# Order of the sums and the statistics in a merge stage, and the first line scan's write-back split by image

## The chip, the cores and the metric

The kernel runs on one core of a Trainium2 chip. Its time is the device time of one execution, in microseconds (us); the figure given for a kernel is the median of several runs. The engines are named as in the profile: PE is TensorE's matrix multiplication (PEld its weight load), DVE is VectorE, ACT is ScalarE, POOL is GpSimd, SP is SyncE, whose queue here issues most transfers (DMA).

## The reference

Four layers work on an fp32 image `x` of shape (2, 128, 128, 128): 2 images, 128 channels, 128 lines, 128 columns. Each normalises its input in groups of 4 channels and adds its result to it. Cut to what matters here:

```
x = x + attention(gn(x))        # layer 0: axial attention, its two outputs scaled, shifted and summed
x = x + scans(gn(x))            # layer 1: four line scans one after the other
x = x + deform_conv(gn(x))      # layer 2
x = x + hadamard_conv(gn(x))    # layer 3

def one_scan(x, w, vertical, reverse):          # layer 1 calls it for down, up, right, left
    def step(carry, xi):
        y = xi + relu(conv1d(carry, w))         # 128 to 128 channels, 9 taps along the line
        return y, y
    _, ys = scan(step, xs[0], xs[1:])           # line by line: each needs the line before it

def gn(v):                                      # mean and variance of 4 channels of one image
    return (g - mean(g)) / sqrt(var(g) + eps)
```

A scan is a chain of 127 steps, each of which depends on the step before. Layer 1's normalisation needs the mean and variance of the whole image that layer 0 leaves, so its first line can't start until the last part of layer 0's sum is there.

## The kernel before, in words

An image stands in SBUF with its 128 channels on the 128 partitions and its lines and columns in the free dimension. Both images are in one tile, `both`, of 128 x 2 x 128 x 128 elements; `res[n]` is image n in it.

**The merge** (`Merge.run`, from line 967) ends layer 0. The attention has written two results to DRAM: `sv`, which is read transposed into tiles `tv`, and `sve`, which is read into tiles `te`. The input is read into `res`. The work is cut into 8 units, 4 for each image, each of 32 columns; a unit has two halves of 16 columns. For a half:

- `add` makes, in two quarters, `u = a0*tv + shift` on ACT (with the transpose in the write) and then `te = a1*te + u` on DVE (`scalar_tensor_tensor`).
- `to_image` adds `te` to the image: lines 0 to 63 on POOL and lines 64 to 127 on DVE, two `tensor_tensor` operations of 1024 elements per partition, with both inputs in SBUF.
- `stats(at, hf, half)` takes the statistics (`bn_stats`) of 2 blocks of 32 lines: half 0 is the blocks that POOL has summed, half 1 the blocks that DVE has summed.

All of these go through `InOrder`, which keeps each engine's instructions in the order in which the program writes them. In a half the program calls `add`, then `stats(*last, 0)` for POOL's lines of the half before, then `to_image`, then `stats(at, hf, 1)` for DVE's own lines. After the last half, `stats(*last, 0)` remains.

The loads go through SP's queue in program order too. There are two `te` tiles and two `tv` tiles. `load_embedded(at + 2)` therefore waits until both sums of unit `at` are done, and `load_sums(at + 1, hf)` until ACT has read the `tv` of unit `at`.

**Layer 1** (`layer1`, from line 1060) first issues 34 DMAs on SP's queue, which store `res`, the image as layer 0 leaves it, to `x1_d` in DRAM (line 1071), in chunks of 8 lines (4 at both ends) of one image each. It then turns the statistics into a scale and a shift and starts the four scans (`d` = 0 to 3). Within a scan a line of 128 columns of both images is kept as two tiles of even and odd columns (`ln0`, `ln1`, each 128 x 2 x 64) and their sum `ln2`. A step does:

1. On PE: three groups of matrix products, `ps[0]` and `ps[1]` and `ps[2]`, from the line before.
2. On ACT: `c0`, a copy of `ps[0]`.
3. On DVE: `v = ps[1] + c0`, then `new[0] = relu(v) + here[0]`, `u`, the second `v`, `new[1]` and `new[2] = new[0] + new[1]`.
4. On ACT, for `d` < 3: the copies `here[k] = new[k]`, which write the finished line back into the image.

`here[k]` is `both[:, :, line, k::2]`: one operand that reaches over both images. In the first scan ACT also normalises lines in place (`normalise(line + 4)`, two operations, one for each image), four lines ahead of the step, before the step's copy `c0`. The `x1_d` stores read the lines before they are normalised, so a normalisation or a write-back of a line has to come after the store that reads it. The framework that builds the program works these waits out from the parts of tiles that operands touch.

Between the stores and the scans, `layer3_weights` is prepared: POOL turns layer 3's weights, once their load (`ta`, issued on SP's queue behind the 34 stores) has landed. In the last scan POOL adds the stored image to the result.

Of the kernel before, what the change touches and what calls it, by code (L numbers as in the profile page):

```python
# [16 lines left out]
N = 2  # L17
# [871 lines left out]
class Merge:  # L889
# [77 lines left out]
    def run(self, prm, res, mv, st_gn):  # L967
        nc, tc = self.env.nc, self.env.tc
        HWC, HS = WC // 2, S // 2
        act, dve, pool = (InOrder(tc, e) for e in (nc.scalar, nc.vector, nc.gpsimd))  # L970
        sp, units = self.sp, self.units
        with ExitStack() as ctx:
            cp = ctx.enter_context(tc.tile_pool(name="mg_c", bufs=1))
            pp = ctx.enter_context(tc.tile_pool(name="mg_ps", bufs=1, space=PSUM))
            for part in range(4):
                self.load_rows(res[0], 0, part)
            a, shift = self.scales(cp, pp, prm, mv)

            def there(at, hf):
                n, wc = units[at]  # L980
                lo = wc * WC + hf * HWC
                return res[n][:, :, lo : lo + HWC]

            HQ = HWC // 2

            def add(at, hf):

                tv = self.sums.pop((at, hf))
                for q in range(2):
                    u = sp.tile([P, S, HQ], F32, name="u", tag="u", bufs=4)  # L990
                    act.activation(
                        u.rearrange("p h w -> p w h"),
                        tv[:, q * HQ : (q + 1) * HQ],
                        AF.Identity,
                        bias=shift,
                        scale=a[:, 0:1],
                    )
                    lo = hf * HWC + q * HQ
                    te = self.embedded[at][:, :, lo : lo + HQ]
                    dve.scalar_tensor_tensor(te, te, a[:, 1:2], u, ALU.mult, ALU.add)  # L1000

            def to_image(at, hf):

                n, wc = units[at]
                te = self.embedded[at][:, :, hf * HWC : (hf + 1) * HWC]
                image = there(at, hf)
                for h, engine in ((0, pool), (HS, dve)):
                    here = image[:, h : h + HS, :]
                    engine.tensor_tensor(here, te[:, h : h + HS, :], here, ALU.add)

            def stats(at, hf, half):
                n, wc = units[at]
                image = there(at, hf)
                for b in (2 * half, 2 * half + 1):
                    dve.bn_stats(
                        st_gn[:, n, wc * NB + hf * 4 + b, :], image[:, b * 32 : (b + 1) * 32, :]
                    )

            last = None
            for at in range(len(units)):
                for hf in range(2):
                    if at > 0:
                        add(at, hf)
                        if at + 1 < len(units):
                            self.load_sums(at + 1, hf)
                    elif hf == 0:
                        for k in range(2):  # L1030
                            add(0, k)
                            self.load_sums(1, k)
                        self.load_rows(res[1], 1, 0)
                        self.load_rows(res[1], 1, 1)
                    if last is not None:
                        stats(*last, 0)
                    last = at, hf
                    to_image(at, hf)
                    stats(at, hf, 1)
                if at + 2 < len(units):  # L1040
                    self.load_embedded(at + 2)
                if at in (0, 1):
                    self.load_rows(res[1], 1, at + 2)
            stats(*last, 0)


# [13 lines left out]
def layer1(env, prm, res, both, x1_d, x1c_d, st_gn, st_next, first, prepare):  # L1060
# [6 lines left out]
    HS = S // 2  # L1067
    with ExitStack() as ctx:
# [17 lines left out]
        for pair in lines:  # L1086
            for t in pair:
                nc.vector.memset(t, 0.0)
        pe, dve, act, pool = (
            InOrder(tc, e) for e in (nc.tensor, nc.vector, nc.scalar, nc.gpsimd)  # L1090
        )
# [8 lines left out]
        def load_columns(w0):  # L1100
            t = xp.tile([P, N, S, CB], F32, name="x1t", tag="x1t")
            nc.sync.dma_start(out=t, in_=x1c_d[w0 // CB])
            return t

        def stats(t, n):
            dve.bn_stats(st_next[:, n, t, :], both[:, n, :, t * RT : (t + 1) * RT])
# [16 lines left out]
        for d in range(4):  # L1123
            steps = list(range(S)) if d % 2 == 0 else list(range(S - 1, -1, -1))
            wl, ws = weights[d]
            if d == 3:
                columns = {w0: load_columns(w0) for w0 in (S - CB, S - 2 * CB)}
            for at, line in enumerate(steps):
                here = [
                    both[:, :, line, k::2] if d < 2 else both[:, :, k::2, line] for k in range(2)  # L1130
                ]
                if d == 0 and line + ahead < S:
                    normalise(line + ahead)
                last, now = lines[turn], lines[1 - turn]
                turn = 1 - turn
                new = [t[:, :, 2 : 2 + HS] for t in now]
                if d == 3:
                    w0 = line // CB * CB
                    if line == w0 + CB - 1 and CB <= w0 < S - CB:
                        columns[w0 - CB] = load_columns(w0 - CB)  # L1140
                    add = [columns[w0][:, :, k::2, line - w0] for k in range(2)]
                if at == 0:
                    for k in range(2):
                        dve.tensor_copy(new[k], here[k])
                    dve.tensor_tensor(new[2], new[0], new[1], ALU.add)
                    if d == 3:
                        for k in range(2):
                            pool.tensor_tensor(here[k], new[k], add[k], ALU.add)
                    continue
                ps = [  # L1150
                    pp.tile([P, N, HS + (k == 1)], F32, name=f"pl{k}", tag=f"pl{k}")
                    for k in range(3)
                ]
                for k in range(3):
                    taps = 4 if k == 1 else 5
                    for j in range(taps):
                        if k == 0 or (k == 2 and j == 0):
                            w = wl[:, 2 * j, :]
                        elif k == 1:
                            w = wl[:, 2 * j + 1, :]  # L1160
                        else:
                            w = ws[:, j - 1, :]
                        pe.matmul(
                            ps[k],
                            lhsT=w,
                            rhs=last[k][:, :, j : j + HS + (k == 1)],
                            start=(j == 0),
                            stop=(j == taps - 1),
                        )
                c0 = sp.tile([P, N, HS], F32, name="c0", tag="c0")  # L1170
                u = sp.tile([P, N, HS], F32, name="u", tag="u")
                v = sp.tile([P, N, HS], F32, name="v", tag="v")
                act.copy(c0, ps[0])
                dve.tensor_tensor(v, ps[1][:, :, 0:HS], c0, ALU.add)
                dve.scalar_tensor_tensor(new[0], v, 0.0, here[0], ALU.max, ALU.add)
                dve.tensor_tensor(u, ps[1][:, :, 1 : HS + 1], c0, ALU.add)
                v = sp.tile([P, N, HS], F32, name="v", tag="v")
                dve.tensor_tensor(v, ps[2], u, ALU.subtract)
                dve.scalar_tensor_tensor(new[1], v, 0.0, here[1], ALU.max, ALU.add)
                dve.tensor_tensor(new[2], new[0], new[1], ALU.add)  # L1180
                if d < 3:
                    for k in range(2):
                        act.copy(here[k], new[k])
                    continue
                for k in range(2):
                    pool.tensor_tensor(here[k], new[k], add[k], ALU.add)
                if line % RT >= 2 and line < S - RT:
                    stats(line // RT + 1, RT - 1 - line % RT)
# [955 lines left out]
```

## Time and profile before

| | |
|---|---|
| time, median of 3 runs | 5569.03 us (5565.35 to 5571.29) |
| the profiled execution's own time | 5575.76 us |
| its span in the profile | 5574.0 us |
| busy: PE, DVE, ACT, POOL | 94%, 66%, 46%, 27% of the span |
| merge | from 1960 to 2103 us of the span |
| the scans | from 2109 to 3765 us |

Times inside the profile are us from the start of the span. A line of the timeline gives the start, the duration, the engine, the line of the code (L81 is the helper `InOrder`, through which most operations go), the operation, what it writes and what it reads, the shapes, how many operations of the kind follow each other without anything else, and in brackets how long the engine had been idle and what ended that. `x_d` is `x1_d`. A line of a group's table gives the busy time, the mean duration of one operation in ns, and the idle time ahead of them with what ended it.

### The profile page before, as it was taken

The page shows a single profiled execution, that of the slowest core. Times are in us where ns is not written, and L with a number is a line of the kernel's source. Part 1 is how long each engine was busy: PE and PEld are TensorE (multiplying, and loading weights), DVE is VectorE, ACT ScalarE, POOL GpSimd, SP SyncE. Part 2 cuts the span into 40 slices and gives each one's busy share as a digit, 9 for nine tenths or more (in the row PEclk, how much of TensorE's full clock was granted, in tenths as well). Part 3 has the DMA queues.
Part 4 walks back from the last instruction along what each step waited for, and adds up shares of the span by engine and source line. Part 5 has one row for each costly group of instructions (what it writes and reads, how often), then busy time and mean ns, then how long its engine had stood idle before and what let it go on. Part 6 is the DMA issues. An engine that isn't in the chain of part 4 may idle for free. (4 is left out here: it accounts for less than half of the span.)

```text
span 5574.0 us, 171601 instructions
## 1 busy us (share of the span) xinstructions
PE 5231.2 (94%) x71931; PEld 4656.9 (84%) x71931; DVE 3700.6 (66%) x7132; ACT 2582.8 (46%) x7864; POOL 1532.4 (27%) x1169
## 2 busy tenths in 40 slices
PE   7997999999999806999999999999899999999999
PEld 6866888888888706999999999993699999999877
DVE  3635888888888875555555556663466666666798
ACT  1056988898889743443223330003233333333322
POOL 2114666666666621000000003330000000000376
PEclk8998999999999958999999999999999999999999
DMA  3353333333333389900000000104576777766211
GB/s 152 108 221 85 60 60 60 60 60 61 60 60 63 95 338 186 100 1 1 1 1 1 1 1 32 47 16 119 113 87 89 88 85 88 90 88 88 44 50 58
DMA packets 673352, 420.99 MB, mean 76 GB/s; under 512 B 325696, under 2 KB 630720, under 8 KB 660672
## 3 DMA queue, kind: packets, MB, share of 16 engines
q1 hardware_dynamic: 667406, 400.69, 38.9%
q8 instruction: 576, 9.44, 0.7%
q10 hardware_dynamic: 5170, 9.23, 0.5%
q14 instruction: 200, 1.64, 0.1%
HBM read 269.09 MB, written 157.45 MB: 77 GB/s over the span
## 5 line engine op out<-in xcount | busy, mean ns | idle before, releaser
L81 PE MATMUL pl<-ln,wl 128*128 128x128 f32 (+1 forms) x10160 | 1243.3, 276 | 31.3 <-DVE ln L81 29.9
L81 PEld LDWEIGHTS pl<-ln,wl 128*128 128x128 f32 x10160 | 1178.4, 191 | 43.8 <-ACT c L81 21.3
L81 ACT ACTIVATE e<-e,mx 128x128 f32<-128x128 f32 x2048 | 793.4, 395 | 0.8 <-DVE mx L81 0.8
L81 ACT COPY sm<-ps_s 128x432 f32<-128x432 f32 (+1 forms) x768 | 318.4, 487 | 834.1 <-PE ps_s L81 808.8
L81 POOL TENSOR_TENSOR e<-e,total 128x1024 f32<-128x1024 f32 x256 | 485.8, 1897 | 485.5 <-DVE total L81 474.8
L81 ACT COPY res<-ln 128x128 f32<-128x128 f32 x762 | 261.8, 344 | 747.0 <-DVE ln L81 722.0
L81 DVE COPY s<-ps_w 100x1152 f32<-100x1152 f32 x256 | 346.4, 1353 | 334.6 <-PE ps_w L81 334.6
L81 PE MATMUL ps_s<-s,xw 100*128 100x144 f32 x4096 | 546.8, 287 | 7.6 <-DMA xw<-px_d 7.6
L81 POOL TENSOR_TENSOR res<-ln,x1t 128x128 f32<-128x128 f32 x256 | 149.1, 583 | 1456.0 <-DVE ln L81 1456.0
L81 PE MATMUL po<-sm,wdef 128*128 128x256 f32 x2304 | 539.1, 379 | 0.0
L81 PE MATMUL pl<-ln,ws 128*128 128x128 f32 x4064 | 537.6, 274 | 0.0
L81 POOL COPY et<-et 128x1024 f32<-128x1024 f32 x256 | 516.8, 2019 | 34.9 <-DVE et L81 25.7
L81 PEld LDWEIGHTS ps_s<-s,xw 100*128 100x128 f32 x4096 | 518.7, 191 | 8.2 <-DMA xw<-px_d 8.0
L81 DVE TENSOR_TENSOR v<-pl,c 128x128 f32<-128x128 f32 x508 | 148.0, 291 | 564.8 <-PE pl L81 542.3
L81 PEld LDWEIGHTS pl<-ln,ws 128*128 128x128 f32 x4064 | 495.5, 191 | 0.0
L81 ACT ACTIVATE r<-gen,alphas 128x1536 f32<-128x1536 f32 x256 | 395.0, 1543 | 171.3 <-PE gen L81 142.4
L81 PEld LDWEIGHTS po<-sm,wdef 128*128 128x128 f32 x2304 | 419.8, 190 | 47.7
L81 POOL MEMSET col<- 128x10 f32 (+1 forms) x72 | 5.9, 122 | 1462.0 <-DVE res L81 1454.6
L81 ACT ACTIVATION_READ_ACCUMULATOR e<-e,mx 128x1 f32 x2048 | 396.2, 193 | 0.0
L81 DVE SCALAR_TENSOR_TENSOR ln<-v,res 128x128 f32<-128x128 f32 x1016 | 346.1, 341 | 48.5 <-POOL res L81 0.9
L81 PE MATMUL te<-cst_main,e 128*128 128x128 f32 x2048 | 337.9, 287 | 28.1 <-POOL e L81 20.6
L81 DVE COPY et<-te 128x512 f32<-128x512 f32 x512 | 348.3, 680 | 13.3 <-PE te L81 13.0
(244 smaller groups left out, 9140.4 us busy)
## 6 DMA issues: line engine op xcount, KB each, us to landing
xw<-px_d SPq DMA_DIRECT2D x1275, 80.0 KB
xa<-in_x SPq DMA_DIRECT2D x16, 1024.0 KB
v_d<-vs SPq DMA_DIRECT2D x16, 1024.0 KB
qb_d<-sb SPq DMA_DIRECT2D x16, 1024.0 KB
qa_d<-sa SPq DMA_DIRECT2D x8, 2048.0 KB
zz<-qb_d SPq DMA_DIRECT2D x1024, 16.0 KB
vt<-v_d SPq DMA_DIRECT2D x64, 256.0 KB
qk<-qa_d SPq DMA_DIRECT2D x256, 64.0 KB
```

Of the source, the lines that this page charges most:

```text
L81: return lambda *a, **k: self.tc.keep_in_program_order(issue(*a, **k))
```

## The change

Three edits. In `to_image` the loop names DVE's half ahead of POOL's, so that the program writes the two sums in that order. In the loop over the halves the statistics of POOL's lines of the half before move from ahead of the sums to behind the statistics of DVE's own lines. In the first scan the write-back of a line is four copies of 128 x 64 elements, one for each image and each of the even and the odd columns, in the place of two copies of 128 x 128 elements that reach over both images; the other scans keep the two.

```
@@ to_image
-                for h, engine in ((0, pool), (HS, dve)):
+                for h, engine in ((HS, dve), (0, pool)):
                     here = image[:, h : h + HS, :]
                     engine.tensor_tensor(here, te[:, h : h + HS, :], here, ALU.add)
@@ the loop over units and halves
+                    to_image(at, hf)
+                    stats(at, hf, 1)
                     if last is not None:
                         stats(*last, 0)
                     last = at, hf
-                    to_image(at, hf)
-                    stats(at, hf, 1)
@@ layer1, end of a step
                 dve.tensor_tensor(new[2], new[0], new[1], ALU.add)
+                if d == 0:
+                    for k in range(2):
+                        for n in range(N):
+                            act.copy(res[n][:, line, k::2], new[k][:, n])
+                    continue
                 if d < 3:
                     for k in range(2):
                         act.copy(here[k], new[k])
```

More of the change, by code (lines that the diff above doesn't have):

```diff
@@ L1006, in to_image @@
                 image = there(at, hf)
-                for h, engine in ((0, pool), (HS, dve)):
+                for h, engine in ((HS, dve), (0, pool)):
                     here = image[:, h : h + HS, :]
@@ L1034, in run @@
                         self.load_rows(res[1], 1, 1)
+                    to_image(at, hf)
+                    stats(at, hf, 1)
                     if last is not None:
@@ L1037, in run @@
                     last = at, hf
-                    to_image(at, hf)
-                    stats(at, hf, 1)
                 if at + 2 < len(units):
@@ L1180, in layer1 @@
                 dve.tensor_tensor(new[2], new[0], new[1], ALU.add)
+                if d == 0:
+                    for k in range(2):
+                        for n in range(N):
+                            act.copy(res[n][:, line, k::2], new[k][:, n])
+                    continue
                 if d < 3:
```

## The prediction

> **What bounds the kernel now.** The engines' shares of the span (PE 94%) say only that PE bounds the whole; both edits lie in places where PE stands still, so I read the waits first and then the timeline there. ACT's groups with their waits, first:
>
> ```profile
> L81 ACT COPY res<-ln 128x128 f32<-128x128 f32 x762 | 261.8, 344 | 747.0 <-DVE ln L81 722.0 <-DMA x_d<-res 24.9
> ```
>
> Of all the write-backs, one waited 24.9 us for the stores to `x1_d`. The timeline around it, engines mixed:
>
> ```profile
> 2116.74 2.40 PE L81 MATMUL pl<-ln,wl 128*128 128x128 f32 x20
> ...
> 2138.91 0.50 ACT L81 COPY res<-ln 128x128 f32<-128x128 f32 x2 [24.95 <-DMA x_d<-res]
> ...
> 2140.37 0.29 DVE L81 TENSOR_TENSOR v<-pl,c 128x128 f32<-128x128 f32 x1 [22.48 <-ACT c L81]
> ...
> 2141.14 4.64 PE L81 MATMUL pl<-ln,wl 128*128 128x128 f32 x20 [21.11 <-DVE ln L81]
> ```
>
> The first line's write-back stands in ACT's queue ahead of the second line's `c0`; DVE waits for `c0`, PE for DVE. The whole scan stops, and the same 20 products then take 4.64 us, not 2.40. The wait is for stores of other lines: `here[k]` reaches from image 0's line into image 1, over everything between.
>
> In the merge, DVE's timeline for one half:
>
> ```profile
> 2058.61 2.46 DVE L81 SCALAR_TENSOR_TENSOR te<-te,a_out,u 128x1024 f32<-128x1024 f32 x2
> 2060.99 1.28 DVE L81 BATCH_NORM_STATS2 st_gn<-res 128x6 f32<-128x512 f32 x2
> 2062.18 2.45 DVE L81 TENSOR_TENSOR res<-te,res 128x1024 f32<-128x1024 f32 x1
> 2064.66 1.29 DVE L81 BATCH_NORM_STATS2 st_gn<-res 128x6 f32<-128x512 f32 x2
> 2065.87 2.46 DVE L81 SCALAR_TENSOR_TENSOR te<-te,a_out,u 128x1024 f32<-128x1024 f32 x2
> ```
>
> No idle time: from 2016 to 2101 DVE is busy 84.0 of 85 us, 7.27 us a half. Its sum takes 2.45 us, but while POOL stood still, the same sum took half:
>
> ```profile
> 1983.49 1.23 DVE L81 TENSOR_TENSOR res<-te,res 128x1024 f32<-128x1024 f32 x1 [11.79 <-DMA res<-in_x]
> ```
>
> POOL's timeline has the reason: its sum starts 0.08 us after `te` ends at 2061.07, and holds DVE's back until about 2063.55.
>
> ```profile
> 2061.15 2.40 POOL L81 TENSOR_TENSOR res<-te,res 128x1024 f32<-128x1024 f32 x1 [4.87 <-DVE te L81]
> ```
>
> **What the Trainium skill says.** "SBUF — State Buffer", section "Who interferes with whom": a DVE instruction with two SBUF inputs and a GpSimd one that reads SBUF exclude each other, whoever issues first keeps the port for the whole instruction; a DVE instruction with one SBUF input isn't touched. The trace agrees: 2.45 against 1.23 us for the sum, and the statistics beside POOL's sum take 1.28 for two, as without it. "TensorE: Matmul & The Clock Gate", section "What's actually happening": an array left idle runs at half clock until some 3.4 us of work have passed; here 4.64 against 2.40 us. "ScalarE: Activation LUTs", section "What ACT_TABLE_LOAD costs": 186 ns + 0.833 ns an element with immediate operands, overlapping by 93 ns back to back. That gives 293 ns for a copy of 128, where the trace has 310 and a spacing of 210.
>
> **The merge, worked out.** Let S be the end of a half's `te`. Before: statistics and then the sum, held by POOL, ends at S+3.56 (2064.63); the next `te` starts at S+4.80. After: DVE's sum needs nothing but `te` and its own image part, and follows `te` on its own engine; dependent operations there start 0.03 to 0.04 us after each other (sum ended 1984.72, its statistics began 1984.75), POOL 0.08 after. So DVE gets the port first. The last scan has this very race, one DVE result releasing both:
>
> ```profile
> 3503.08 0.29 DVE L81 TENSOR_TENSOR ln<-ln,ln 128x128 f32<-128x128 f32 x1
> 3503.12 0.63 POOL L81 TENSOR_TENSOR res<-ln,x1t 128x128 f32<-128x128 f32 x1 [0.55 <-DVE ln L81]
> ```
>
> DVE keeps its 0.29, POOL has 0.63 where it has 0.53 alone. DVE's sum thus ends at S+1.26, four statistics (2.47, as at 1984.75, the next operation overlapping by 0.08) bring S+3.67, and with `te` (2.46) a half takes 6.13 us. POOL's sum, pushed behind, ends at S+1.25+2.40 = S+3.65, just as the next `te`, which wants the port too, starts. What POOL's lateness touches: the statistics moved behind read the half before, long done; the next `te` load waits for both sums, at S+3.65 where it was S+3.56.
>
> The gain counts only where DVE bounds. Until 2026.4 ACT waits for `tv` loads (1985.8, 2011.3, 2026.4), with DMA moving 405 GB/s: nothing there. Unit 3's `te` ends at 2030.72+1.29 = 2032.0 in both versions. Nine halves later it was 2097.40; now 2032.0+9x6.13 = 2087.2. The loads must keep up: a unit moves 4.2 MB, 10.2 us at 410 GB/s, against 12.3 us. The latency is tighter: `te` issued 2042.9, ACT had `tv` at 2052.6, 9.7 us later, and `u` takes 2.2; against that stand 12.3 us. Unit 5, whose load waits for unit 3, misses by some 0.6 us; later ones fit. So 2087.8. The tail: before, the statistics ended at S+6.08 (2103.48); after, the last pair waits for POOL and ends at S+3.65+0.08+1.28 = S+5.0, 2092.8. **Gain 10.7 us.** If the loads bind fully at about 13.3 us a unit, half of it goes; if POOL got the port first, DVE would end its sum at S+3.6 and then do four statistics: 8.5 us a half, a loss of about 11.
>
> **The write-back, worked out.** The instruction orders of both builds, with their waits, show this: PE, POOL and SP keep their order. The waits for five DMA semaphores on the first write-back are gone; in their place, a normalisation waits for its own line's chunk, once in 8 lines. A chunk pair is 1 MB, 2.6 us at 404 GB/s (2101 to 2140), and 8 steps are 25 us, so those waits are met. The first chunks of image 1 are issued when POOL's last sum ends, now about 2091.4; the first normalisation comes 5.5 us after the statistics (2103.48 to 2108.96), at 2098.3. That is 6.9 us, where `wl`, of like size, took 5.6 from issue (2101.20) to use (2106.80).
>
> Without the stop, line 2's `v` would follow PE's start by 2.28, as in steady state (2403.79 to 2406.07): 2119.0 in place of 2140.37, 21.35 us. Line 3's `v` then came at 2145.81, 5.44 on, where a step is 3.13: the cold array costs 2.3 more. **Gain 23.65 us.** POOL's turning of the weights (2143 to 2161) slows about five steps to 3.57; it will meet other steps, at equal cost.
>
> The price: 127 steps with two more ACT operations. The steady state of the first scan:
>
> ```profile
> 2404.64 0.31 ACT L81 COPY res<-ln 128x128 f32<-128x128 f32 x1 [0.74 <-DVE ln L81]
> 2404.85 0.88 ACT L81 ACTIVATE res<-res,gb_l,gs_l 128x128 f32<-128x128 f32 x2
> 2405.63 0.24 ACT L81 COPY c<-pl 128x128 f32<-128x128 f32 x1
> 2406.07 0.29 DVE L81 TENSOR_TENSOR v<-pl,c 128x128 f32<-128x128 f32 x1 [1.14 <-PE pl L81]
> ```
>
> `c0` is done at 2405.87 and `v` waits for PE until 2406.07: 0.17 us of cover, less 0.03 for the signal. PE is busy 372.3 of 374 us there. The even columns' copies fall into ACT's idle 0.74. The odd ones' push normalisation and `c0` by one spacing less the smaller size: an estimate from the ScalarE page is 146 ns a copy of 64, so 2x146-210 = 82 ns. Covered. Were a copy of 64 as dear as one of 128, the push is 210 ns: 0.04 to 0.07 over, 5 to 9 us in 127 steps; at no push, nothing. I take 0.4 us.
>
> **Sum.** 10.7 + 23.65 - 0.4 = 34 us. The profiled execution (5575.76, span 5574.0) would come to 5542; it lies 6.7 above the median, so I take the gain off the median: 5569 - 34 = **5535 us**.
>
> **Rivals.** (a) POOL wins the port: for it, the sum is then issued to an idle engine; against, the last scan. 5569 + 11 - 23.3 = 5557, still faster by a hair. (b) The merge turns to waiting for loads and gives half or less: 5540 to 5546. (c) ACT bounds the first scan, at 0.05 to 0.15 us a step: 5541 to 5554. (d) Slower: the same mechanism as (c), at the four copies of a step; it decides from 34/127 = 0.27 us a step, 0.14+0.27 = 0.41 push, so 0.31 us between starts of 64-element copies where copies of twice the size have 0.21. At 0.4 us the push is 0.59, 0.45 above the cover, 57 us in 127 steps: 5535 + 57 = 5592. Nothing in the profile speaks for it. (e) The edit does nothing to the stop, because a normalisation then waits as long: the chunk arithmetic speaks against; 5558.
>
> **Chances.** Main case 0.71, with its own range 5529 to 5541; (a) 0.07, (b) 0.09, (c) 0.07, (e) 0.03, (d) 0.03. The range 5528 to 5552 holds the main case, (b) and most of (c). About 0.2%, 11 us, is what a measurement of this kernel can tell from no change: faster by more 0.92; within it 0.04, from the edges of (a) and (e); slower 0.04.
>
> **What would show it.** DVE's sum at about 1.23 us and POOL's at up to 3.6; a half at 6.1; statistics done near 2093; no ACT wait on `x_d` of 20 us; one cold start of PE; first-scan steps at 3.13. I am wrong if DVE's sum stays at 2.4, if `v` waits for ACT instead of PE, or if an early normalisation waits for a store.

## The result and the profile after

| | before | after |
|---|---|---|
| time, median (5 runs each) | 5570.67 us (5565.35 to 5574.83) | 5539.68 us (5532.62 to 5542.76) |
| ratio | | 0.994, 95% interval 0.9929 to 0.9951 |
| span of the profiled execution | 5574.0 us | 5537.9 us |

The change saves 31.0 us in the medians (27 to 40 by the interval) and 36.1 us in the two spans. The moment at which the attention ends, before anything that the change touches, is not the same in every execution: it lay between 1953.6 and 1962.7 us in the twelve profiles of this study. All comparisons of traces below therefore count from one mark, the start of the last `BATCH_NORM_AGGREGATE` on `mv_out`, which closes the attention. Lines of a scan are counted as in the prediction, from the first one that a step makes.

| counted from the mark, us | before | after | gain |
|---|---|---|---|
| last statistics done (start of the aggregate on `mv_l`) | 145.27 | 134.50 | 10.8 |
| `v` of the third line of the first scan | 187.68 | 151.85 | 35.8 |
| `v` of the last line of the last scan | 1805.38 | 1770.45 | 34.9 |

So all of the gain is there when the third line of the first scan begins, and the 505 steps behind it keep it to within 1 us.

**The merge after**, in DVE's timeline for one half and the first quarters of the next (start, duration, engine, line, operation, output and inputs, shapes, count, and idle time ahead with what ended it):

```profile
2046.62 2.47 DVE L81 SCALAR_TENSOR_TENSOR te<-te,a_out,u 128x1024 f32<-128x1024 f32 x2
2049.12 1.23 DVE L81 TENSOR_TENSOR res<-te,res 128x1024 f32<-128x1024 f32 x1
2050.38 2.47 DVE L81 BATCH_NORM_STATS2 st_gn<-res 128x6 f32<-128x512 f32 x4
2052.77 1.27 DVE L81 SCALAR_TENSOR_TENSOR te<-te,a_out,u 128x1024 f32<-128x1024 f32 x1
2054.22 1.28 DVE L81 SCALAR_TENSOR_TENSOR te<-te,a_out,u 128x1024 f32<-128x1024 f32 x1 [0.18 <-ACT u L81]
```

and in POOL's:

```profile
2049.17 3.45 POOL L81 TENSOR_TENSOR res<-te,res 128x1024 f32<-128x1024 f32 x1 [2.70 <-DVE te L81]
```

DVE's sum starts first and takes 1.23 us where it took 2.45. POOL's is now the longer one, 3.45 us where it took 2.40, and DVE doesn't wait for it: DVE's next two operations that need the same port start at 2052.77, 0.15 us after POOL's end. From `te` to `te` a half takes 6.15 us (2046.62 to 2052.77). The last line of DVE's view is the first sign of the loads: 0.18 us of waiting for `u`.

**The start of the first scan after**, engines mixed:

```profile
2098.38 4.02 PE L81 MATMUL pl<-ln,wl 128*128 128x128 f32 x20 [3.70 <-DVE ln L81]
...
2102.29 0.29 DVE L81 TENSOR_TENSOR v<-pl,c 128x128 f32<-128x128 f32 x1 [2.62 <-PE pl L81]
...
2103.13 2.40 PE L81 MATMUL pl<-ln,wl 128*128 128x128 f32 x20
...
2105.42 0.29 DVE L81 TENSOR_TENSOR v<-pl,c 128x128 f32<-128x128 f32 x1 [1.14 <-PE pl L81]
```

The second line's `v` follows the first's by 3.13 us (24.87 before). PE starts cold once, at 4.02 us for 20 products, and in the second line they take 2.40. ACT's write-backs, in its groups by shape (busy us, mean ns of one, then the idle time ahead and what ended it), no longer wait for any store:

```profile
L81 ACT COPY res<-ln 128x128 f32<-128x128 f32 x508 | 183.4, 361 | 514.3 <-DVE ln L81 514.3
L81 ACT COPY res<-ln 128x64 f32<-128x64 f32 x508 | 100.5, 247 | 187.0 <-DVE ln L81 187.0
```

The first row is the other scans' 508 copies. The second is the 508 copies of half the size, 247 ns each. In the steady first scan the second pair of them stands ahead of the normalisation and `c0`:

```profile
2405.74 0.39 ACT L81 COPY res<-ln 128x64 f32<-128x64 f32 x2 [0.65 <-DVE ln L81]
...
2406.82 0.24 ACT L81 COPY c<-pl 128x128 f32<-128x128 f32 x1
...
2407.17 0.29 DVE L81 TENSOR_TENSOR v<-pl,c 128x128 f32<-128x128 f32 x1 [1.13 <-PE pl L81]
```

Two copies take 0.39 us together and one takes 0.247, so their starts lie 0.15 us apart. `c0` ends at 2407.06 and `v` still waits for PE, until 2407.17. A step of the steady scan is 3.13 us, as before.

### The profile page after: what moved, and what is told of

It reads as the page before. It is cut to its first block, busy times and chain, and to the rows that moved or that the text cites. A ratio compares the mean times of both kernels' runs of the same rounds, so it can differ in the third digit from the quotient of the medians.

```text
span 5537.9 us, 171854 instructions
## 1 busy us (share of the span) xinstructions
PE 5230.7 (94%) x71931; PEld 4656.8 (84%) x71931; DVE 3687.8 (67%) x7132; ACT 2604.6 (47%) x8118; POOL 1546.4 (28%) x1169
## 5 line engine op out<-in xcount | busy, mean ns | idle before, releaser
L81 ACT COPY res<-ln 128x64 f32<-128x64 f32 (+1 forms) x1016 | 283.9, 304 | 701.2 <-DVE ln L81 701.2
```

What stands on the lines that cost most here:

```text
L81: return lambda *a, **k: self.tc.keep_in_program_order(issue(*a, **k))
```

## The experiments

Each kernel is the changed one with the edit shown, unless another base is named. Time is the median; the ratio is to the kernel before, measured beside it, with its 95% interval. That kernel's own median went from 5570.67 to 5577.44 us from one group of runs to the next, so kernels of different groups are compared by their ratios. Statistics, third line and last line are counted from the mark.

| | time, us | ratio | statistics | third line | last line | one half |
|---|---|---|---|---|---|---|
| before | 5570.67 | | 145.27 | 187.68 | 1805.38 | 7.27 |
| the change | 5539.68 | 0.994 (0.9929 to 0.9951) | 134.50 | 151.85 | 1770.45 | 6.15 |
| the change again | 5540.57 | 0.9942 (0.9929 to 0.9956) | 134.92 | 153.03 | 1770.87 | 6.15 |
| split write-back alone | 5547.95 | 0.9957 (0.9944 to 0.9971) | 145.10 | 163.75 | 1781.95 | 7.27 |
| merge alone | 5568.91 | 0.9989 (0.9982 to 0.9995) | 134.64 | 179.62 | 1797.50 | 6.15 |
| POOL's sum named first | 5543.25 | 0.9948 (0.9934 to 0.9961) | 135.14 | 152.51 | 1770.30 | 6.15 |
| stores image by image | 5548.83 | 0.9958 (0.9944 to 0.9971) | 134.88 | 158.76 | 1776.73 | 6.15 |
| both sums on DVE | 5547.62 | 0.9945 (0.9931 to 0.996) | 144.17 | 163.08 | 1777.73 | 7.16 |
| one block ahead | 5558.49 | 0.9969 (0.9957 to 0.998) | 151.76 | 170.33 | 1788.38 | 7.86 |
| eight copies | 5544.84 | 0.9942 (0.9928 to 0.9956) | 135.09 | 153.08 | 1776.31 | 6.15 |
| split in 16 lines only | 5542.05 | 0.9935 (0.992 to 0.9949) | 135.00 | 153.21 | 1770.73 | 6.15 |
| `u` in PSUM, POOL takes 96 lines | 5533.44 | 0.9924 (0.991 to 0.9938) | 128.54 | 146.60 | 1764.58 | 5.60 |

The theory was that two stalls go, each in its own place: DVE's sum no longer waits for POOL's, since it is issued first, and the first write-back no longer waits for stores of other lines. The rivals to be told apart were that POOL keeps the port, that the write-back's wait turns up elsewhere, and that the four copies slow the scan.

**The split write-back alone** (the kernel before, with this edit):

```
+                if d == 0:
+                    for k in range(2):
+                        for n in range(N):
+                            act.copy(res[n][:, line, k::2], new[k][:, n])
+                    continue
```

> The write-back split alone, the merge as before. The two parts meet at one place only, the start of the stores, so they should add. Theory (a false wait of one copy on the stores of other lines): the copy's wait of 25 us goes, PE starts cold once, 23 us faster than before: ratio 0.9958, some 5547. Rival (the gain came mostly from the merge, and the stop only grows shorter with it): less than 12 us faster, ratio above 0.998.

The median is 26.9 us under that of the kernel before, measured beside it (5574.85). In the trace the statistics are where they were (145.10), and from there to the third line it is 18.65 us where it was 42.41: the stop is worth 23.76 us by itself.

**The merge alone** (the change without that block):

> The order of sums and statistics alone, the write-back as before. Theory: a half of 6.1 us in the steady part, the statistics done some 11 us earlier; the stop at the first write-back stays, its end moving with the stores, which start when the last sum of GpSimd ends, 9 to 11 us earlier: 10 us faster, ratio 0.998. Rival (the stores end when they did, because the DMAs bind): no faster, and the copy's wait grows from 25 to 35 us.

It gained 5.9 us in the median, with an interval of 3 to 10, and 7.9 us in the trace at the last line, for statistics that are 10.6 us earlier. ACT's timeline has the difference:

```profile
2128.61 0.50 ACT L81 COPY res<-ln 128x128 f32<-128x128 f32 x2 [27.62 <-DMA x_d<-res]
```

The first write-back waited 24.95 us before, and waits 27.62 now. It is the stores that it waits for, and the stores of image 1 start when POOL's last sum ends. POOL's last sum starts 9.5 us earlier than before but now takes 3.44 us in place of 2.41, so that it ends 8.5 us earlier (133.29 for 141.77). The statistics gain 10.6, because they end 1.35 us behind it where they ended 3.50. The stop then ends 8.0 us earlier (172.74 for 180.78). While the stop is there, the merge's gain ahead of it counts only as far as it moves the stores. That is most of why the parts alone give 23.4 and 7.9 us at the last line and both together 34.9: at the third line it accounts for 2.6 of the 3.8 us that are missing. The other 1.3 is in the start of the scan, which takes longer with the split alone (18.65 us for 17.35) and is taken up below.

**POOL's sum named first:**

```
-                for h, engine in ((HS, dve), (0, pool)):
+                for h, engine in ((0, pool), (HS, dve)):
```

> The change with its first edit undone: GpSimd's half named ahead of VectorE's in the loop. The two sums go to different queues and touch different lines. Theory: the edit moves nothing on any engine, and the time is that of the change, 5540 within 6 us, VectorE's sum at 1.22 us, a half at 6.15 us; all of the merge's gain is from the statistics moved. Rival (naming it first is what wins the port): VectorE's sum at 2.4 us and more, the merge 10 us or more longer.

DVE, ACT and POOL run the same operations in the same order in both kernels, so this is the change run once more: 5543.25, half 6.15. The first of the three edits does nothing. DVE and POOL have queues of their own, and which of the two sums is written first in the program puts neither ahead of the other. The merge's whole gain comes from the statistics that no longer stand between `te` and DVE's sum.

**One block of statistics ahead of the sums**, the other behind:

```
-            def stats(at, hf, half):
+            def stats(at, hf, half, which=(0, 1)):
-                for b in (2 * half, 2 * half + 1):
+                for b in [2 * half + w for w in which]:
...
+                    if last is not None:
+                        stats(*last, 0, (0,))
                     to_image(at, hf)
                     stats(at, hf, 1)
                     if last is not None:
-                        stats(*last, 0)
+                        stats(*last, 0, (1,))
```

> The change with one of the two statistics blocks put back ahead of VectorE's sum: VectorE is busy with it for 0.6 us while GpSimd starts. Theory (whoever issues first keeps the port): VectorE's sum begins 0.6 us after te, reads 3 us long, and ends 3.6 us after te; with 3 statistics behind it a half takes 3.6 + 1.85 + 2.45 = 7.9 us, longer than before the change (7.27) though only 0.6 us of work moved: some 15 us slower than the change, 5555. Rival (the two share the port, or the moved statistics themselves bring the gain): a half between 6.1 and 7.3 us, 5540 to 5550.

The timelines of DVE and POOL:

```profile
2047.84 0.69 DVE L81 BATCH_NORM_STATS2 st_gn<-res 128x6 f32<-128x512 f32 x1
2048.00 2.40 POOL L81 TENSOR_TENSOR res<-te,res 128x1024 f32<-128x1024 f32 x1 [5.46 <-DVE te L81]
2048.44 3.04 DVE L81 TENSOR_TENSOR res<-te,res 128x1024 f32<-128x1024 f32 x1
2051.52 1.88 DVE L81 BATCH_NORM_STATS2 st_gn<-res 128x6 f32<-128x512 f32 x3
```

A block of 0.6 us ahead of the sum is enough: POOL's sum starts beside that block, DVE's comes 0.44 us after it and takes 3.04 us, and a half 7.86. DVE's sum ends 3.6 us after `te` here as it did before the change, but then two of the half's four blocks were done while POOL held the port, and here one. Of no, one and two blocks ahead of DVE's sum, one is the dearest (6.15, 7.86 and 7.27 us a half). The time is 16.4 us over that of the kernel with the split in 16 lines, which was measured beside it.

**Both sums on DVE:**

```
-                for h, engine in ((HS, dve), (0, pool)):
+                for h, engine in ((HS, dve), (0, dve)):
```

> The change with GpSimd's sums given to VectorE. Theory (two sums exclude each other at the port, so before the change GpSimd's sum took from VectorE all the time that it saved): a half takes 2.46 + 2x1.22 + 2.4 = 7.3 us as before the change, the merge ends about 10 us later than with the change, 5550. Rival (VectorE was slowed by something else than GpSimd, such as its place behind the statistics): a half clearly off 7.3 us, above 8 or below 6.5.

```profile
2049.05 2.36 DVE L81 TENSOR_TENSOR res<-te,res 128x1024 f32<-128x1024 f32 x2
```

In DVE's timeline the two sums take 2.36 us together, and a half 7.16. The kernel before, with POOL doing one of them, had 7.27: POOL's help saved DVE nothing there, since DVE's own sum was held for 1.22 us, as long as a second sum takes. The statistics are 9.7 us later than in the change, as expected. At the last line only 7.3 of this are left. The first scan is 2.5 us shorter than the change's (390.32 us from the third line to the last, for 392.79) and the last scan 1.4 (411.93 for 413.30). The traces show where: in every other kernel each 16th step of the first scan, from the one to the third line on, takes 3.48 us in place of 3.13, and six steps of the last scan take 3.6. Here no such step is in the first scan and two are in the last. Why is open.

**Stores image by image, with the wide write-back of before:**

```
-        for lo, hi in [(0, 4)] + [(h, h + 8) for h in range(4, S - 4, 8)] + [(S - 4, S)]:
-            for n in range(N):
+        for n in range(N):
+            for lo, hi in [(0, 4)] + [(h, h + 8) for h in range(4, S - 4, 8)] + [(S - 4, S)]:
```

> The merge as changed, the write-back not split (two copies over both images), and the stores issued image by image: all 17 of image 0 and then the 17 of image 1. Theory (the copy waits for the stores of the stretch from its line in image 0 to its line in image 1, that is nearly all of image 0): image 0 is complete in the middle of the merge, so its stores are done before the scan starts, and the stop is gone without the split: the copy's wait under 2 us, time that of the change, 5540 within 6 us. Rival (the copy waits for every store, of image 1 too): the stop stays, wait 20 us or more, about 5560.

This kernel leaves the two wide copies as they are and issues all of image 0's stores first, so that the lines between the two ends of a copy are stored before the scan begins. ACT's timeline:

```profile
2105.28 4.34 ACT L81 ACTIVATE res<-res,gb_l,gs_l 128x128 f32<-128x128 f32 x11 [5.86 <-DMA x_d<-res]
...
2110.98 0.31 ACT L81 COPY res<-ln 128x128 f32<-128x128 f32 x1 [1.22 <-issue]
```

The last line is the first write-back, and it waits for no store, although SP goes on issuing stores of image 1 until 2120. So its wait was for the stretch of image 0 between its two ends, as the prediction had it, and not for every store. The time was not as expected: image 1's first chunk is now 18th in the queue, and the first normalisation of image 1 waits 5.86 us for it, with DMA moving 398 GB/s from 2072 to 2105. The third line comes 6.9 us later than in the change, and the median is 5.6 us over that of POOL's sum named first, measured beside it. The wait moved from the write-back to the normalisation, at a quarter of its size.

**Eight copies a step in the first scan:**

```
-                            act.copy(res[n][:, line, k::2], new[k][:, n])
+                            for c in range(2):
+                                act.copy(
+                                    res[n][:, line, 64 * c + k : 64 * c + 64 : 2],
+                                    new[k][:, n, 32 * c : 32 * c + 32],
+                                )
```

> The change with eight copies of 32 elements in the place of four of 64 in the first scan, to find where the price of more copies begins. A copy of 64 shows a spacing of 0.145 us; one of 32 should show 0.12. Theory: the odd columns' four copies push normalisation and c0 by 0.48 - 0.29 = 0.19 us more than the change does; of cover the change has left 0.08 us, so a step grows by about 0.1 us in the most, 127 steps: up to 13 us slower than the change, 5540 to 5553, v waiting for ACT and steps of 3.2 us. Rival (ACT is far from the path): steps stay 3.13, 5540.

Timeline, ACT and DVE:

```profile
2404.85 0.58 ACT L81 COPY res<-ln 128x32 f32<-128x32 f32 x4 [0.45 <-DVE ln L81]
...
2406.39 0.29 DVE L81 TENSOR_TENSOR v<-pl,c 128x128 f32<-128x128 f32 x1 [1.25 <-ACT c L81]
```

Now `v` waits for ACT's `c0`: in 122 of the 127 steps of the scan, where it is 5 in the change (all while POOL turns layer 3's weights) and 1 before. In the mean a step takes 3.21 us, for 3.17 in the change, and the scan 397.76, 5.2 us more than the mean of the change's two profiles (392.54). The same doubling from two copies to four cost nothing that shows. ACT begins to set the step's length somewhere between four copies and eight; with 0.11 us of cover left at four (2407.06 to 2407.17), it could not take much more.

**The split in the first 16 lines only:**

```
-                if d == 0:
+                if d == 0 and line < 16:
```

> The change with the split write-back for lines 1 to 15 alone, and the two wide copies for the 112 lines after them, when all stores are done. Theory (two more copies a step are covered in full): no difference to the change beyond 3 us, 5540, steps 3.13 us in both stretches. Rival (the four copies cost up to 0.05 us a step): 3 to 6 us faster than the change.

The scan takes 392.10 us where the change's two profiles have 392.79 and 392.29, and the kernel before 392.29. The price of four copies over the whole scan is at most 0.7 us, and no difference shows in the times.

**`u` in PSUM and three quarters of the sum on POOL**, and **the change again** beside it:

```
+        te = self.sp.tile([P, S, WC], F32, name="te", tag="te", bufs=3)
-                    u = sp.tile([P, S, HQ], F32, name="u", tag="u", bufs=4)
+                    u = pp.tile([P, S, HQ], F32, name="u", tag="u", bufs=3)
-                for h, engine in ((HS, dve), (0, pool)):
+                for lo, hi, engine in ((96, S, dve), (0, 96, pool)):
-                for b in (2 * half, 2 * half + 1):
+                for b in ((0, 1, 2), (3,))[half]:
```

> The change, with u in PSUM (three buffers), a third te tile in the room that this frees, and GpSimd summing 96 lines of 128. Theory (the port is contended only by a VectorE operation with two SBUF inputs, so te, with u in PSUM, may overlap GpSimd's sum): GpSimd's sum reads some 4.2 us and runs on beside the next te, which keeps 2.46 us for two; VectorE's sum of 32 lines takes 0.65 us, a half 5.5 us, and the loads keep up with three te tiles: the statistics end some 6 us earlier than with the change, 5534. Rival (te is held by GpSimd all the same): te starts or ends only when GpSimd's sum ends, a half 6.6 us, 4 us slower than the change.

> The change itself, beside it on the same chip: 5540 within 6 us, a half 6.15 us.

With `u` in PSUM, `te` has one input in SBUF instead of two, and so should not need the port that POOL holds. POOL may then work on into `te`, and take more of the sum. Timeline, DVE and POOL:

```profile
2049.19 2.45 DVE L81 SCALAR_TENSOR_TENSOR te<-te,a_out,u 128x1024 f32<-128x1024 f32 x2
...
2051.72 4.02 POOL L81 TENSOR_TENSOR res<-te,res 128x1536 f32<-128x1536 f32 x1 [1.58 <-DVE te L81]
...
2054.79 2.46 DVE L81 SCALAR_TENSOR_TENSOR te<-te,a_out,u 128x1024 f32<-128x1024 f32 x2
```

POOL's sum runs until 2055.74, 0.95 us into the `te` of the next half, which takes its 2.46 us all the same. That it would have been held with `u` in SBUF is not shown on `te` itself, since in no other kernel does POOL's sum meet one; the same operation on two elements with all inputs in SBUF, `gb_l`, was held by POOL at the start of the scan (0.69 us for 0.16, in the change again). A half takes 5.60 us, the statistics are 6.4 us earlier than in the change run beside it and the last line 6.3 us. The medians say 7.1 us less, 5533.44 for 5540.57; their two intervals overlap, so it is the traces that show the gain. Three things changed at once here, and the gain is not divided among them: the third `te` tile or a shorter `u` may have a part in it, since the waits that lengthen three of the change's later halves by up to 0.3 us are gone too. This is the fastest kernel of the study, 41 us under the one before, measured beside it (5574.46).

## Why the prediction was right, and where it was off

**The merge** was right in mechanism and size: DVE's sum 1.23 us, POOL's ending 3.53 us after `te` (3.65 predicted), a half 6.15 (6.13), the statistics 10.8 us earlier (10.7). The race for the port goes as the last scan's did. That issue order decides it is shown by the block put ahead, and that the price of losing is real too: the sum then took 3.04 us. Rival (a) did not occur, and that run shows the like of its cost: 7.86 us a half, with one block less behind the sum than in rival (a), which had 8.5. The loads, rival (b), cost about what the sum had for them, but not where it had it: the first halves of units 5, 6 and 7 are 0.26, 0.13 and 0.30 us longer than 6.15, where the sum had 0.6 us at unit 5 and none later.

**The stop** was right in mechanism. Its size was 25.06 us in the change's profile (42.41 from the statistics to the third line before, 17.35 after), where the sum had 21.35 + 2.3 = 23.65. Both terms were a little off. The second line's `v` came 0.39 us sooner than worked out. Of the third line's 5.43 us only 1.95 could go and not 2.3, because its step takes 3.48 us and not 3.13 without the stop too: it is the first of the 16th steps named with both sums on DVE. These two errors cancel, which is luck.

What is left is a term that the sum did not have: it took the beginning of the scan, from the statistics to the first products, as the same in both kernels. It is not. The timelines there, engines mixed, of before:

```profile
2106.80 1.28 POOL L1056 TENSOR_TENSOR ws<-wl 128x512 f32<-128x512 f32 x1 [5.31 <-DMA wl<-in_wscan]
...
2107.01 1.08 DVE L67 TENSOR_TENSOR gs_l<-gm_l,sq_l 128x2 f32<-128x2 f32 x1
...
2109.70 1.26 POOL L1056 TENSOR_TENSOR ws<-wl 128x512 f32<-128x512 f32 x1 [1.62 <-DMA wl<-in_wscan]
2109.87 1.31 DVE L81 COPY ln<-res 128x128 f32<-128x128 f32 x2 [0.95 <-ACT res L81]
```

and of after:

```profile
2095.13 1.27 POOL L1057 TENSOR_TENSOR ws<-wl 128x512 f32<-128x512 f32 x1 [4.57 <-DMA wl<-in_wscan]
...
2095.31 1.12 DVE L44 TENSOR_SCALAR gs_l<-gs_l 128x2 f32<-128x2 f32 x1
...
2098.01 0.36 DVE L81 COPY ln<-res 128x128 f32<-128x128 f32 x2 [0.95 <-ACT res L81]
...
2098.25 1.27 POOL L1057 TENSOR_TENSOR ws<-wl 128x512 f32<-128x512 f32 x1 [1.85 <-DMA wl<-in_wscan]
```

It is the port of the merge once more. POOL adds up the scans' weights as their loads land, 1.27 us a piece, and short DVE operations on the path to the first product stand still meanwhile. Before, the subtraction on two elements took 1.08 us (0.13 in the change) and the two copies 1.31 (0.36): twice 0.95 us. After, only `gs_l` is caught ahead of the first product, 1.12 us for the 0.17 it has before, and the second POOL sum starts 0.24 us behind the copies instead of 0.17 ahead of them. From the statistics to PE's first product it is 7.79 us before and 6.84 after; less what was held (1.90 and 0.95) it is 5.89 in both. The others agree: the split alone has 7.99 with 1.10 and 0.99 held, the change again 6.42 with 0.53 held, and all nine other profiles in which no normalisation waits for a store leave 5.83 to 5.90. Among these it goes with the merge and not with the split: the seven profiles with the merge as changed, or with `u` in PSUM besides, have 6.40 to 6.93 us, the other four 7.21 to 7.99.

"SBUF — State Buffer" in the Trainium skill, section "Who interferes with whom", names these operations: a copy or an operation with a scalar can enter a mode that takes both ports, and one with two SBUF inputs needs the shared one. The trace agrees, with the copies and the operation with a scalar held here. The prediction read that section for the merge alone, and its short form, by which an operation with one input in SBUF isn't touched, leaves this exception out, as does the "only" in the expectation for `u` in PSUM.

Of the 1.4 us that the stop gained beyond the sum, 0.95 is this. Another 0.40 lies between PE's first product and the first `v`, 4.31 us before and 3.91 after. That and the 0.39 of the second line are PE's cold start, which differs from one execution to the next (4.06 us to the first `v` and 3.13 from there to the second in the split alone, 4.32 and 3.90 in the change again), and the change has no part in it that any run shows. In the repeats the stop's gain comes to 24.3 (the change again) and 25.0 us (POOL's sum named first).

**The write-back's price** was right: 0.15 us between starts (146 ns estimated), `v` still waits for PE, and the run with the split in 16 lines saves at most 0.7 us. Rivals (c) and (d) were the right thing to watch, since eight copies do turn the bound. Rival (e), a normalisation that waits instead, did not happen here; with the stores in another order it did, for 5.86 us.

**The time** was 5535 predicted and 5540 measured. Of the 4.7 us between, 1.6 is the base, which was 5569 in three runs and is 5570.67 in five. The sum of 34 us lies between the medians' gains (31.0, and 31.6 and 33.9 us in the two repeats) and the traces' (34.5 to 35.1 at the last line). How much of the remaining 3 us is the spread of the attention's end, some 9 us between profiles, can't be told from medians of 5 runs.

## What to carry to other kernels

When two engines share a port, count the work that stands between the common result and each engine's next use of the port: on the engine that should win it should be nothing, for one short operation was worse here than two. A wait that ends at one engine is a sum of everything that holds it, so look for the same lock wherever both engines are awake, small operations on a start-up path included. And an operand that reaches over two images brings in the waits of all that lies between: write it in two pieces where that stalls, and see how much room the engine that does it has left.

## What the runs showed of the hardware that was not expected

- ACT's transposing write of `u` costs 1.20 us into PSUM and 2.22 into SBUF, the same operation otherwise. Groups by shape, the change's and then that of `u` in PSUM:

```profile
L81 ACT ACTIVATE u<-tv,shift,a_out 128x1024 f32<-128x1024 f32 x32 | 66.0, 2217 | 57.2 <-DMA tv<-sv_d 56.1 <-DVE shift L964 1.0
```

```profile
L81 ACT ACTIVATE u<-tv,shift,a_out 128x1024 f32<-128x1024 f32 x32 | 37.8, 1202 | 76.3 <-DMA tv<-sv_d 60.8 <-DVE te L81 10.8 <-DVE st_gn L81 3.2
```

  It was moved for the sake of the port. No run shows whether the steps of the write or something else in SBUF makes the difference.
- An operation on 2 elements takes 0.67 to 1.27 us in place of 0.12 to 0.17, when it falls behind a POOL sum.
- The loser of the port ends a little sooner than the two times in a row would have it. POOL's sum, 2.40 us alone, ends 2.27 us after DVE's (2050.35 to 2052.62, after the change); DVE's, 1.23 alone, ends 1.08 after POOL's (2050.40 to 2051.48, with one block ahead).
